# A five-layer graph network on one core: products of the second neighbour sum made within the stretch of the first

## The chip, the core and the metric

The kernel runs on one core of one Trainium2 chip. The metric is the device time of one execution in microseconds, given as the median of the runs shown; lower is better. A profile is one execution recorded by the hardware profiler, and all times from the trace count from its first instruction.

## The reference, cut to what matters

A graph has N = 6250 nodes with 128 features each and E = 106250 directed edges, sorted by destination. Four blocks follow one another, each added to its input and normalised. The change lies in the first block, two mean convolutions:

```python
def _sage_conv(h, src, dst, Wl, bl, Wr):
    msgs = h[src]
    agg = jax.ops.segment_sum(msgs, dst, num_segments=N)
    deg = jax.ops.segment_sum(jnp.ones((src.shape[0],), h.dtype), dst, num_segments=N)
    agg = agg / jnp.maximum(deg, 1.0)[:, None]
    return agg @ Wl.T + bl + h @ Wr.T
...
h = jax.nn.relu(_sage_conv(x, src, dst, W1l, b1l, W1r))
return _sage_conv(h, src, dst, W2l, b2l, W2r)
```

and then `x = _layernorm(x + ...)`. The second block has one symmetric convolution, the third has two, and the fourth has three layers of three weighted hops, each a sum over neighbours with the edges' weights.

## The kernel before, in words

**Sums as dense products.** Nodes are cut into NW = 49 windows of 128. A neighbour sum is a product of node features with a matrix of counts: for a destination, how many edges come from each source. Destinations are taken in NC = 13 chunks, six of 4 windows, three of 3 and four of 4 (RUNS, SHAPE, START: 0, 4, 8, 12, 16, 20, 24, 27, 30, 33, 37, 41, 45). For chunk c, `counted_sum` (L462) walks over the 49 source blocks: it loads the chunk's columns of counts seven blocks at a time on SP's queue (`columns`, L450), casts them from bytes to fp32r two blocks at a time (L478) and multiplies each block with the features. Features are kept as a high and a low part, so each block costs two matmuls (L489) of 512 columns, or 384 for a chunk of three windows. The sum grows in one PSUM bank (`accumulator`, two buffers).

**Where counts come from.** GpSimd writes them. For each of 49 blocks of edge records, `cell` (VectorE) works out the cells and values, and `scatter` (L551) issues 17 indirect DMAs (L555). A chunk's columns may be loaded once the blocks of edges near it have been scattered (`columns` makes the load wait for them). GpSimd's order is written out: `in_line` puts each scatter behind the one before it, first all counts (833), then the matrix of edge weights for the hops (578, L733 to L735), then 48 fetches of edges (`gathered_edges`, L752).

**First sum** (L701 to L731). For each chunk: the next chunk's cells are prepared, degrees are counted (L654), `counted_sum` runs with x's parts (t0hi, t0lo), all casts on ScalarE, and `mean_conv` (L529) turns the sum into h: the sum times w1l, divided by the degree, plus x times w1r, plus the bias; then ReLU, and `split` into t1hi and t1lo. Its argument `also` makes part of the second sum on the way: with the same columns, it adds the products of t1 with the source blocks below START[c], which are known by then (tile `half`, L721 to L725); they are stored in `halves[c]`.

**Second sum** (L777 to L790). Chunk by chunk, with the columns loaded and cast a second time, the source blocks from START[c] on are summed, `evicted` (L496) adds `halves[c]`, and `mean_conv` makes the second convolution: it adds up t1hi and t1lo to h, turns h (`turned`, four transposes, L416, and a copy on ScalarE, L418), multiplies by w2r (`times`, L424) and adds. Then x is added (tile xr, loaded whole by `load_nodes` at L773 on ScalarE's queue), the result is normalised and the next table (t2) is made. Casts alternate between VectorE and ScalarE (`turns`): of seven blocks VectorE takes four.

**Third, fourth and fifth sum** (L811, L829, L842) work in the same way, over all 49 blocks. In the fifth, after chunk c's hop table (L850), `gathered_edges` is called for two windows (L852): GpSimd fetches their edges into tiles gm and ge (L757), and six small VectorE instructions (L761 to L766) unpack them. Those six are held behind L850's instruction of that chunk, so that none comes earlier.

**Hops** (from L1036). Nine hops, whose TensorE order is written out by a planner (class Stream, with costs and due times); part of the destinations go through dense products with the weights' matrix (L1030), the rest through rows that GpSimd gathers (L962).

**What sets the order elsewhere.** Outside the hops a scheduler orders each engine's instructions when the program is built: what is ready by its own reckoning goes first, in the order of the program among those. On the chip each engine then keeps to that order.

Of the kernel before, what the change touches and what calls it, by code (L numbers as in the profile page):

```python
# [360 lines left out]
def usual_way(ctx, tc, a, out, dram, ident, part, first, recs, edges, counts, weights, fills, empty):  # L361
# [97 lines left out]
    def accumulator():  # L459
        return ps_acc.tile([P, CW], F32, name="acc")  # L460

    def counted_sum(pool, c, parts, turns, own=False, wide_bufs=3, slots=None, since=0, also=None):  # L462


        cw, acc, todo, t = width(c), accumulator(), [], None
        step = STEPS
        for s in range(since, NW):
            r = (s - since) % step
            if r == 0:
                t = next(slots) if slots is not None else pool.tile([P, step * CW], U8, name="cols", tag="cols")  # L470
                t = columns(t, c, counts, U8, step, s)
            if not todo:
                n, engine = turns[0]
                turns.append(turns.pop(0))
                wide = pool.tile([P, n * CW], FR, name=f"wide{engine}", tag=f"wide{engine}", bufs=wide_bufs)
                n = min(n, step - r)
                copy = nc.vector.tensor_copy if engine == "v" else nc.scalar.copy
                copy(wide[:, :n * cw], t[:, r * cw:(r + n) * cw])  # L478
                todo = [wide[:, i * cw:(i + 1) * cw] for i in range(n)]
            if own and s == NW - 1:  # L480
                for j, w in enumerate(windows_of(c)):
                    for lhs in parts(w):
                        nc.tensor.matmul(acc[:, j * P:(j + 1) * P], lhs, identr[:], start=False, stop=False)
            cols = todo.pop(0)
            for into, of_block, begin, end in [(acc, parts, since, NW)] + ([also] if also else []):
                if s < end:
                    lhss = of_block(s)
                    for i, lhs in enumerate(lhss):
                        nc.tensor.matmul(into[:, :cw], lhs, cols, start=s == begin and i == 0,  # L489
                                         stop=s == end - 1 and i == len(lhss) - 1)  # L490
        return acc
# [29 lines left out]
    def both(hi, lo):  # L521
        return lambda s: [hi[:, s, :], lo[:, s, :]]

    halves = {c: dram.tile([P, width(c)], F32, name=f"half{c}") for c in range(1, NC)}

    def of(c):
        return SHAPE[c], slice(START[c], START[c] + SHAPE[c])

    def mean_conv(c, acc, wl, wr, bias, hi, lo, more=None):  # L529
        n, ws = of(c)  # L530
        x = new("h", n)
        nc.vector.tensor_add(x[:], hi[:, ws].bitcast(F32), lo[:, ws].bitcast(F32))
        agg = evicted(acc, width(c), more)
        po = times(n, agg, wl)
        y = new("y", n)
        nc.vector.tensor_tensor(y[:], po, per_node(invdeg, ws, D), op=ALU.mult)
        px = times(n, turned(x), wr)
        nc.vector.tensor_add(y[:], y[:], px)
        nc.vector.tensor_add(y[:], y[:], per_feature(bias, n))
        return y  # L540


    queue = []
# [28 lines left out]
    with tc.tile_pool(name="counted", bufs=2) as counted, tc.tile_pool(name="cells", bufs=1) as cells, \  # L572
# [138 lines left out]
        for c in range(NC):  # L711
            n, ws = of(c)
            fetch_chunk(c + 2)
            if c + 4 < NC:
                empty(counts, U8, c + 4, nc.sync)
            count_cells(c + 1)
            for i in sorted(i for i in blocks_near(c) if i in degs):
                degrees(i)
            norms(c)
            also = None  # L720
            if c > 0:  # L721
                also = ps_half.tile([P, CW], F32, name="half"), both(t1hi, t1lo), 0, START[c]
            acc = counted_sum(counted, c, both(t0hi, t0lo), [(2, "s")], slots=slots, also=also)
            if c > 0:
                nc.scalar.dma_start(halves[c][:], evicted(also[0], width(c))[:, :width(c)])  # L725
            y = mean_conv(c, acc, wt["w1l"][:], wt["w1r"][:], wt["b1l"], t0hi, t0lo)
            h = new("h", n)
            nc.vector.tensor_scalar_max(h[:], y[:], 0.0)
            split(t1hi[:, ws], t1lo[:, ws], h[:])
            if c < ND:  # L730
                empty(weights, F32, c, nc.sync)  # L731

# [37 lines left out]
    nc.vector.tensor_copy(wt["wk"][:, 12], ident[:])  # L770
    turns = [(2, "v"), (2, "s"), (2, "v"), (1, "s")]
    xr = tabs.tile([P, NW, D], F32, name="xr", tag="xr")
    load_nodes(nc.scalar, xr, slice(0, NW))  # L773
    with tc.tile_pool(name="counted2", bufs=2) as counted:
        t2 = table("t2", 0, FR)
        slots = columns_room("room1")
        for c in range(NC):  # L777
            n, ws = of(c)
            half = None
            if c > 0:  # L780
                half = sums_room()
                nc.scalar.dma_start(half[:, :width(c)], halves[c][:])
            acc = counted_sum(counted, c, both(t1hi, t1lo), turns, slots=slots, since=START[c])
            y = mean_conv(c, acc, wt["w2l"][:], wt["w2r"][:], wt["b2l"], t1hi, t1lo, half)
            nc.vector.tensor_add(y[:], y[:], xr[:, ws])
            norm(xr[:, ws], y)
            pm = times(n, turned(xr[:, ws]), wt["wconv"][:], DH)
            u = new("u", n, DH)
            nc.vector.tensor_tensor(u[:], pm, per_node(dinv, ws, DH), op=ALU.mult)
            split(t2[:, ws, :DH], t2[:, ws, DH:], u[:])  # L790


        def sym_conv(c, sums, bias, d=D):
            n, ws = of(c)
            r = new("y", n, d)
            nc.vector.tensor_tensor(r[:], sums, per_node(dinv, ws, d), op=ALU.mult)
            nc.vector.tensor_add(r[:], r[:], per_feature(bias, n))
            return r


        def next_parts(c, hi, lo, x):
            n, ws = of(c)
            u = new("u", n)
            nc.vector.tensor_tensor(u[:], x, per_node(dinv, ws, D), op=ALU.mult)
            split(hi[:, ws], lo[:, ws], u[:])

        def summed(c, parts, w):
            return times(SHAPE[c], evicted(counted_sum(counted, c, parts, turns, own=True), width(c)), w)

        t3 = table("t30", 2, FR), table("t31", 3, FR)  # L810
        for c in range(NC):  # L811
            n, ws = of(c)
            agg = evicted(counted_sum(counted, c, lambda s: [t2[:, s, :]], turns, own=True,
                                      slots=slots), width(c))
            pr = bank()
            for j in range(n):
                nc.tensor.matmul(pr[:, j * DH:(j + 1) * DH], agg[:, j * P:(j + 1) * P], stacked[:],
                                 start=True, stop=True)
            r = sym_conv(c, pr[:, :n * DH].rearrange("p (n d) -> p n d", d=DH), wt["bconv"], DH)
            nc.vector.tensor_scalar_max(r[:], r[:], 0.0)  # L820
            po = times(n, turned(r, DH), wt["wlin"][:])
            y = new("h", n)
            nc.vector.tensor_tensor(y[:], po, per_feature(wt["blin"], n), op=ALU.add)
            nc.vector.tensor_add(y[:], y[:], xr[:, ws])
            norm(xr[:, ws], y)
            next_parts(c, *t3, xr[:, ws])

        t4 = table("t40", 0, FR), table("t41", 1, FR)
        for c in range(NC):  # L829
            n, ws = of(c)  # L830
            r = sym_conv(c, summed(c, both(*t3), wt["g1"][:]), wt["gb1"])
            nc.vector.tensor_scalar_max(r[:], r[:], 0.0)
            next_parts(c, *t4, r[:])


        hop_out, hid = table("hop", 2), table("hid", 3)
        stored = [dram.tile([P * NW, D], F32, name=f"stored{i}") for i in range(2)]

        def store(ws, i, t):
            nc.scalar.dma_start(stored[i].rearrange("(p w) d -> p w d", p=P)[:, ws, :], t[:, ws])  # L840

        for c in range(NC):  # L842
            n, ws = of(c)
            r = sym_conv(c, summed(c, both(*t4), wt["g2"][:]), wt["gb2"])
            nc.vector.tensor_add(r[:], r[:], xr[:, ws])
            norm(xr[:, ws], r)
            po = times(n, turned(xr[:, ws]), wt["wk"][:, 0])
            nc.vector.tensor_tensor(hid[:, ws], xr[:, ws], per_feature(wt["bias0"], n), op=ALU.add)
            nc.vector.tensor_add(hid[:, ws], hid[:, ws], po)
            last = nc.vector.tensor_tensor(hop_out[:, ws], xr[:, ws], per_node(dinvw, ws, D), op=ALU.mult)  # L850
            store(ws, 0, hop_out)
            for i in range(2 * c, min(2 * c + 2, NG)):  # L852
                gathered_edges(i, last.ins)
# [549 lines left out]
```

## Time and profile before

| what | value |
|---|---|
| median of 3 runs | 8167.57 us (8165.88 to 8180.15) |
| the profiled execution, its own time | 6165.89 us |
| its span in the trace | 6164.0 us |
| TensorE busy, share of the span | 5392.1 us, 87% |
| GpSimd busy | 4296.6 us, 70% |
| VectorE / ScalarE busy | 3117.1 us / 2142.5 us |
| first sum, to its last eviction | 1254.1 us |
| second sum, from its first unbroken products to its last eviction | 1283.5 to 1476.7 us |
| last scatter of weights begins | 2020.45 us |
| first product of the hops, about | 2316 us |

The profiled execution took 2001.7 us less than the median of the runs; its span doesn't show why. Lines of the profile read as follows. A group names the line, the engine and the operation, then tiles written and read, then a count. PE is TensorE, PEld its weight load, DVE VectorE, ACT ScalarE, POOL GpSimd, SP the engine that only issues DMAs; a q behind a name means the engine's sequencer, which issues DMAs or waits. A line of waits reads: who waited, for whom, microseconds in total, times, the longest.

### The profile page before, as it was taken

The page shows a single profiled execution, that of the slowest core. Times are in us where ns is not written, and L with a number is a line of the kernel's source. Part 1 is how long each engine was busy: PE and PEld are TensorE (multiplying, and loading weights), DVE is VectorE, ACT ScalarE, POOL GpSimd, SP SyncE. Part 2 cuts the span into 40 slices and gives each one's busy share as a digit, 9 for nine tenths or more (in the row PEclk, how much of TensorE's full clock was granted, in tenths as well). Part 3 has the DMA queues.
Part 4 walks back from the last instruction along what each step waited for, and adds up shares of the span by engine and source line. Part 5 has one row for each costly group of instructions (what it writes and reads, how often), then busy time and mean ns, then how long its engine had stood idle before and what let it go on. Part 6 is the DMA issues. An engine that isn't in the chain of part 4 may idle for free.

```text
span 6164.0 us, 74568 instructions
## 1 busy us (share of the span) xinstructions
PE 5392.1 (87%) x20184; PEld 3336.0 (54%) x20184; DVE 3117.1 (51%) x8599; ACT 2142.5 (35%) x4396; POOL 4296.6 (70%) x4207
## 2 busy tenths in 40 slices
PE   1356655889999999999999999999999999999998
PEld 0234443567788784555554555554545555545555
DVE  8274544247955664434445544434355444344466
ACT  1233322445855452323323323323233233233233
POOL 4777777777877306767767747767677477677676
PEclk9688877999999999999999999999999999999999
DMA  9367871154644448999998889999988899998997
GB/s 280 107 189 243 237 194 46 46 147 125 187 130 135 135 136 295 307 308 313 307 316 287 286 287 318 305 312 308 309 299 289 283 320 304 312 310 298 325 319 248
DMA packets 710710, 1525.52 MB, mean 247 GB/s; under 512 B 134918, under 2 KB 344196, under 8 KB 710020
## 3 DMA queue, kind: packets, MB, share of 16 engines
q1 hardware_dynamic: 535728, 1292.14, 62.6%
q0 software_dynamic: 134496, 181.90, 11.0%
q10 hardware_dynamic: 40052, 46.61, 2.2%
q8 instruction: 160, 2.62, 0.2%
q14 instruction: 274, 2.24, 0.1%
HBM read 1332.27 MB, written 187.93 MB: 247 GB/s over the span
## 4 chain that ended last, share of the span: by engine, by line
PE 33%; DMA 27%; POOL 15%; issue 14%; DVE 9%; ACT 2%; POOLq 0%; ACTq 0%; DVEq 0%; SPq 0%
DMA rows<-stored,gsrc 25%; PE acc L1030 20%; POOL weights L555 7%; PE acc L489 5%; POOL counts L555 5%; POOL rows L962 3%; PE gacc L998 2%; ACT both L994 2%; DVE both L995 2%; PE pp L424 1%; PE pd L654 1%; PE half L489 1%; DVE oh L653 1%; PE pp L886 1%; DMA slots<-counts 1%
## 5 line engine op out<-in xcount | busy, mean ns | idle before, releaser
L962 POOL DMA_INDIRECT rows<-stored,gsrc x2736 | 2720.3, 994 | 1229.5 <-issue 348.1
L1030 PE MATMUL acc<-weighed,hop 128*128 128x512 f32 (+1 forms) x7938 | 3492.3, 560 | 2.8 <-DMA weighed<-weights 2.8
L994 ACT ACTIVATE both<-rows,gwgt 128x128 fp32r<-128x128 f32 x2736 | 1075.3, 400 | 2461.1 <-DMA rows<-stored,gsrc 1588.6
L995 DVE SCALAR_TENSOR_TENSOR both<-rows,gwgt,both 128x128 fp32r<-128x128 f32 x2736 | 947.9, 351 | 1876.4 <-ACT both L994 1866.1
L1030 PEld LDWEIGHTS acc<-weighed,hop 128*128 128x128 f32 x7938 | 1326.7, 191 | 988.2 <-issue 750.4
L998 PE MATMUL gacc<-both,oh 128*128 128x256 f32 x2736 | 1743.2, 643 | 4.3 <-issue 2.1
L489 PE MATMUL acc<-wides,t 128*128 128x512 f32 (+1 forms) x2929 | 842.0, 392 | 315.7 <-ACT wides L478 315.6
L555 POOL DMA_INDIRECT counts<-cval,celli x833 | 872.3, 1047 | 269.9 <-issue 244.0
L998 PEld LDWEIGHTS gacc<-both,oh 128*128 128x128 f32 x2736 | 521.8, 191 | 585.1 <-issue 300.7
L555 POOL DMA_INDIRECT weights<-wval,celli x578 | 653.8, 1131 | 176.1 <-issue 176.1
L489 PEld LDWEIGHTS acc<-wides,t 128*128 128x128 f32 x2929 | 540.9, 192 | 427.0 <-ACT wides L478 278.9
L478 ACT CAST wides<-slots 128x1024 fp32r<-128x1024 uint8 (+3 forms) x645 | 527.5, 853 | 633.9 <-DMA slots<-counts 408.6
L489 PE MATMUL acc<-widev,t 128*128 128x512 f32 (+1 forms) x2210 | 608.9, 386 | 21.9 <-DVE widev L478 11.8
L978 DVE TENSOR_TENSOR oh<-iota,gdst 128x640 fp32r<-128x640 f16 x576 | 452.6, 786 | 50.3 <-PE gacc L998 43.9
L489 PEld LDWEIGHTS acc<-widev,t 128*128 128x128 f32 x2210 | 408.6, 189 | 102.8 <-DVE widev L478 25.3
L653 DVE TENSOR_SCALAR oh<-iota,dloc 128x384 bf16<-128x384 f16 x833 | 228.8, 336 | 337.9 <-PE pd L654 337.4
L478 ACT CAST wides<-cols 128x512 fp32r<-128x512 uint8 (+1 forms) x364 | 289.7, 797 | 251.9 <-PE acc L489 223.1
L478 DVE CAST widev<-cols 128x1024 fp32r<-128x1024 uint8 (+1 forms) x364 | 247.8, 686 | 236.2 <-DMA cols<-counts 138.2
L654 PE MATMUL pd<-oh,lw 128*4 128x384 bf16 x833 | 185.8, 339 | 66.3 <-DVE oh L653 65.8
L478 DVE CAST widev<-slots 128x1024 fp32r<-128x1024 uint8 (+1 forms) x281 | 188.2, 681 | 52.9 <-PE acc L489 43.1
L489 PE MATMUL half<-wides,t 128*128 128x512 f32 (+1 forms) x594 | 185.9, 393 | 0.0
L424 PE MATMUL pp<-wk,xT 128*128 128x128 f32 x582 | 95.3, 296 | 84.8 <-ACT xT L418 84.8
(230 smaller groups left out, 2734.1 us busy)
## 6 DMA issues: line engine op xcount, KB each, us to landing
weighed<-weights SPq DMA_DIRECT2D x1296, 512.0 KB
weighed<-weights SPq DMA_DIRECT2D x648, 384.0 KB
slots<-counts SPq DMA_DIRECT2D x175, 448.0 KB
weights<-zeros SPq DMA_DIRECT2D x6, 12544.0 KB
cols<-counts SPq DMA_DIRECT2D x140, 448.0 KB
rows<-stored,gsrc POOLq DMA_INDIRECT x2736
counts<-zeros SPq DMA_DIRECT2D x10, 3136.0 KB
weights<-zeros SPq DMA_DIRECT2D x3, 9408.0 KB
```

Of the source, the lines that this page charges most:

```text
L424: nc.tensor.matmul(pm[:, j * d:(j + 1) * d], xt[:, j * P:(j + 1) * P], w, start=True, stop=True)
L478: copy(wide[:, :n * cw], t[:, r * cw:(r + n) * cw])
L489: nc.tensor.matmul(into[:, :cw], lhs, cols, start=s == begin and i == 0, stop=s == end - 1 and i == len(lhss) - 1)
L555: ins = nc.gpsimd.indirect_dma_start(out=mat[:], out_offset=bass.IndirectOffsetOnAxis(ap=celli[:, i, k:k + 1], axis=0), in_=vals[:, i, k:k ...
L653: nc.vector.tensor_scalar(oh[:], iota[:], dloc[:, k:k + 1], None, op0=ALU.is_equal)
L654: nc.tensor.matmul(acc[:], lw[:, k, :], oh[:], start=k == 0, stop=k == KD - 1)
L962: nc.gpsimd.indirect_dma_start(out=fetched_rows[:, self.slot(self.asked), :], out_offset=None, in_=stored[self.h % 2][:], in_offset=bass.I ...
L978: nc.vector.tensor_tensor(oh[:, :m, :], iota[:, :P].unsqueeze(1).to_broadcast([P, m, P]), gdst[:, i, ks].unsqueeze(2).to_broadcast([P, m, ...
L994: nc.scalar.activation(both[:, :D], x, AF.Copy, scale=w)
L995: nc.vector.scalar_tensor_tensor(both[:, D:], x, w, both[:, :D].bitcast(F32), op0=ALU.mult, op1=ALU.subtract)
L998: nc.tensor.matmul(self.acc[:, j * 2 * D:(j + 1) * 2 * D], self.oh[:, k % HOTS, :], both[:], start=k == 0, stop=k == KG - 1)
L1030: nc.tensor.matmul(acc[:, :cw], tables[h][:, s, :], t[:, s % STEP * cw:(s % STEP + 1) * cw], start=s == 0, stop=s == NW - 1)
```

## The change

`counted_sum` gets an end as well as a start (`until`). `mean_conv` loses the own product, which becomes `plus_product`; `fetched_sums` loads a stored partial sum.

In the first sum, each chunk now also makes its part of the second convolution's own product: x + h w2r + b2l, stored in DRAM as `bases[c]`. And after chunks 8, 9, 10 and 11, two more partial sums follow, those of chunks 0 and 1, 2 and 3, 4 and 5, 6 and 7 of the second convolution: source blocks from START[e] up to KNOWN = START[9] = 33, whose t1 is known after chunk 8. `halves[e]` is added, and the result is stored as `early_parts[e]`. Their columns are loaded and cast for it, all casts on ScalarE.

The second sum then starts at block 33 for chunks 0 to 7 (unchanged for chunks 8 to 12), adds what is stored, and loads `bases[c]` into xr chunk by chunk where it had loaded x whole.

```diff
-    def counted_sum(pool, c, parts, turns, own=False, wide_bufs=3, slots=None, since=0, also=None):
+    def counted_sum(pool, c, parts, turns, own=False, wide_bufs=3, slots=None, since=0, until=NW, also=None):
...
-        for s in range(since, NW):
+        for s in range(since, until):
...
-                n = min(n, step - r)
+                n = min(n, step - r, until - s)
...
-            for into, of_block, begin, end in [(acc, parts, since, NW)] + ([also] if also else []):
+            for into, of_block, begin, end in [(acc, parts, since, until)] + ([also] if also else []):
...
+    KNOWN, AHEAD = START[ND], 8
     halves = {c: dram.tile([P, width(c)], F32, name=f"half{c}") for c in range(1, NC)}
+    early_parts = {c: dram.tile([P, width(c)], F32, name=f"early{c}") for c in range(AHEAD)}
+    bases = {c: dram.tile([P, SHAPE[c], D], F32, name=f"base{c}") for c in range(NC)}
...
+    def fetched_sums(part):
+        t = sums_room()
+        nc.scalar.dma_start(t[:, :part.shape[1]], part[:])
+        return t
+
+    def plus_product(y, x, w, bias):
+        n = y.shape[1]
+        nc.vector.tensor_add(y[:], y[:], times(n, turned(x), w))
         nc.vector.tensor_add(y[:], y[:], per_feature(bias, n))
...
-            y = mean_conv(c, acc, wt["w1l"][:], wt["w1r"][:], wt["b1l"], t0hi, t0lo)
-            h = new("h", n)
+            x = new("h", n)
+            nc.vector.tensor_add(x[:], t0hi[:, ws].bitcast(F32), t0lo[:, ws].bitcast(F32))
+            y = mean_conv(c, acc, wt["w1l"][:])
+            plus_product(y, x[:], wt["w1r"][:], wt["b1l"])
+            h = new("u", n)
             nc.vector.tensor_scalar_max(h[:], y[:], 0.0)
             split(t1hi[:, ws], t1lo[:, ws], h[:])
+
+            plus_product(x, h[:], wt["w2r"][:], wt["b2l"])
+            nc.scalar.dma_start(bases[c][:], x[:])
+            for e in range(2 * (c - ND + 1), 2 * (c - ND + 2)):
+                if 0 <= e < AHEAD:
+                    half = fetched_sums(halves[e]) if e > 0 else None
+                    acc = counted_sum(counted, e, both(t1hi, t1lo), [(2, "s")], slots=slots,
+                                      since=START[e], until=KNOWN)
+                    nc.scalar.dma_start(early_parts[e][:], evicted(acc, width(e), half)[:, :width(e)])
...
-    load_nodes(nc.scalar, xr, slice(0, NW))
...
-            half = None
-            if c > 0:
-                half = sums_room()
-                nc.scalar.dma_start(half[:, :width(c)], halves[c][:])
-            acc = counted_sum(counted, c, both(t1hi, t1lo), turns, slots=slots, since=START[c])
-            y = mean_conv(c, acc, wt["w2l"][:], wt["w2r"][:], wt["b2l"], t1hi, t1lo, half)
+            nc.scalar.dma_start(xr[:, ws], bases[c][:])
+            half = fetched_sums(early_parts[c] if c < AHEAD else halves[c])
+            acc = counted_sum(counted, c, both(t1hi, t1lo), turns, slots=slots,
+                              since=KNOWN if c < AHEAD else START[c])
+            y = mean_conv(c, acc, wt["w2l"][:], half)
```

## The prediction

> **What bounds the kernel now.** I read the slices first, then the waits of the first sum, then GpSimd's own waits, then one table of stretches, then the few microseconds in which GpSimd and VectorE meet.
>
> The slices (40 of 154 us each; the digits are tenths busy):
> ```profile
> PE   1356655889999999999999999999999999999998
> POOL 4777777777877306767767747767677477677676
> ```
> TensorE is half idle in slices 0 to 6 and full from slice 9. GpSimd is the reverse: a level 7 without a break up to slice 12, then nothing before the hops. Who waits up to 1290 us:
> ```profile
> ACT wides L478 <- DMA slots<-counts: 408.6, 13, 62.1
> ...
> PE acc L489 <- ACT wides L478: 315.6, 10, 53.0
> ```
> Each chunk of the first sum waits for its counts, which GpSimd scatters. GpSimd itself, up to 1190 us and then from 1850 to 2021 us, waits for nobody; "issue" is its 0.3 us between two instructions:
> ```profile
> POOL counts L555 <- issue: 243.7, 800, 0.3
> POOL counts L555 <- DVE f L636: 16.7, 2, 16.4
> ```
> ```profile
> POOL weights L555 <- issue: 37.8, 124, 0.3
> ```
> So it runs one queue, at its own pace: 833 scatters of counts, 578 of weights, then the 48 fetches of L757. The table of stretches gives that pace (columns: length, then busy and instructions of PE, PEld, DVE, ACT, POOL, then clock, DMA share, GB/s):
> ```profile
> 1254.00:1283.50 29.50, 6.57 (x26) 5.62 (x25) 7.39 (x12) 2.92 (x5) 22.79 (x22) 0.62 0.95 300
> 1283.50:1477.00 193.50, 192.74 (x1009) 162.23 (x1010) 135.28 (x307) 100.79 (x147) 151.45 (x139) 0.99 0.47 132
> 1477.00:1690.00 213.00, 197.37 (x975) 155.61 (x974) 186.73 (x465) 159.99 (x238) 172.77 (x133) 0.96 0.58 167
> 1690.00:2000.00 310.00, 310.00 (x1531) 265.50 (x1530) 174.37 (x275) 163.74 (x218) 242.36 (x223) 1.00 0.47 133
> ...
> 904.50:954.00 49.50, 2.85 (x11) 0.81 (x10) 4.43 (x18) 1.09 (x2) 37.78 (x39) 0.55 0.13 36
> 1003.00:1043.50 40.50, 1.55 (x9) 0.59 (x8) 2.47 (x11) 0.00 (x0) 30.80 (x32) 0.57 0.08 20
> 1104.00:1131.40 27.40, 1.73 (x10) 0.59 (x8) 2.22 (x8) 0.00 (x0) 20.92 (x22) 0.62 0.11 30
> ```
> Row 2 is the second sum, row 3 the third, row 4 the fourth; the last three are the waits for counts that the early products could fill. One scatter takes 193.5 / 139 = 1.39 us, 213 / 133 = 1.60, 310 / 223 = 1.39, and 49.5 / 39 = 1.27 where VectorE rests. Now the meeting, VectorE's timeline in the fifth sum (start, length, instruction, idle before it):
> ```profile
> 2023.31 0.68 DVE L850 TENSOR_TENSOR hop<-xr,dinvw 128x512 f32<-128x512 f32 x1
> 2024.53 0.21 DVE L761 TENSOR_SCALAR gdst<-gm 128x17 f32<-128x17 f32 x1 [0.53 <-DMA gm<-recs,gat]
> ...
> 2027.00 0.23 DVE L764 TENSOR_SCALAR gdst<-ge 128x2 f32<-128x2 f32 x1 [2.11 <-DMA ge<-edges,gat]
> ...
> 2030.79 0.71 DVE L478 CAST widev<-cols 128x1024 fp32r<-128x1024 uint8 x1
> ```
> and GpSimd's:
> ```profile
> 2020.45 1.09 POOL L555 DMA_INDIRECT weights<-wval,celli  x1 [0.30 <-issue]
> 2021.85 0.99 POOL L757 DMA_INDIRECT gm<-recs,gat  x1 [0.30 <-issue]
> ```
> VectorE finishes the fifth sum's first chunk at 2023.3 us and turns to gathered_edges, whose rows GpSimd began to fetch at 2021.85, straight after its last weight. VectorE already loses 5.5 us there and TensorE 3.9. The two chains arrive together: both must be shortened to gain.
>
> **What the Trainium skill says.** "SBUF — State Buffer", section Who interferes with whom: a VectorE instruction in a 2-port mode holds the port pair that it shares with GpSimd for its whole length. The paces agree in direction: 1.27 us with VectorE at rest, 1.60 with it 88% busy. "TensorE: Matmul & The Clock Gate", section Architectural detail: the array is 16× 32×32, not 1× 128×128: ScalarE and VectorE are strictly first in, first out. The trace agrees: at 1043.52 a cast of chunk 10, held 41.6 us by its counts, stands before the eviction of chunk 9 (1044.47). The same page, What's actually happening: an idle TensorE restarts at half clock for a window of about 3.4 us. After a 24.6 us wait, pairs of 384-wide matmuls here come 0.64 us apart for 6 us, then 0.35.
>
> **The change, part by part.**
> *Products moved.* Chunks 0 to 5 have 33, 29, 25, 21, 17, 13 blocks below 33, so 138 blocks, two matmuls each: 276 of width 512; chunks 6 and 7 have 9 + 6 blocks: 30 of width 384. Pairs start 0.46 us apart at full clock (1215.44, 1215.90), 0.23 each; 384-wide 0.35 a pair, 0.173. 276 x 0.229 + 30 x 0.173 = 63.2 + 5.2 = 68.4 us leave the second sum.
> *Own product moved.* In that stretch w2r's matmuls are busy 11.0 us and the transposes of h 6.3: 17.3 us off TensorE, and three of VectorE's 0.69 us operations per chunk (26 us).
> *Second sum.* TensorE 192.7 - 68.4 - 17.3 = 107 us; VectorE 135.3 - 26 - casts for 153 of 340 blocks (71.6 x 0.45 = 32) = 77 us. TensorE stays the limit: 108 us in place of 193.5, a saving of 85.
> *The load of xr goes* (3.2 MB, ScalarE's queue). ScalarE stood from 1254.7 to 1273.6 behind it, which delayed chunk 12's tail; of the 29.5 us hole some 15 go. In its place come 13 loads and 13 stores of 256 KB and 8 stores of partial sums, 0.33 us of ScalarE each, beside TensorE's work.
> *First sum.* Early pairs follow chunks 8, 9, 10, 11: 124, 92, 60, 30 matmuls = 28.4, 21.1, 13.7, 5.2 us, against waits of 46.7, 40.6, 27.3 and none. Casts on ScalarE alone run 0.93 us per two blocks, as fast as the four matmuls need. Only the last 5.2 us and an own product stay uncovered, and chunk 10's tail (4 us) slips into the wait: +3 us. If the early products came behind the next chunk's first matmul in TensorE's order, up to 68 us would be uncovered. 25 more column loads on SP queue behind chunk 8 to 11's; the fetches of recs are all out by 516 us and from the fourth block of records on cells are ready over 60 us before their scatter, so GpSimd's queue isn't starved.
> *Sum so far:* 85 + 15 - 3 = 97 us: L850 of the fifth sum's first chunk moves from 2023.3 to 1926.
> *What is late next: GpSimd.* It gets no instruction less. From 1192: 79.5 us to the second sum's new start (1271.5) at 1.32 = 60 scatters; 108 us at 1.47 (between 1.39 and 1.60: VectorE's share, 77 / 108 = 0.71, is near the 0.70 of before, and I allow for waits that I don't see) = 73; third sum, fourth sum and fifth's first chunk 370. At 1926 some 578 - 503 = 75 are left; at 1.27 they take 96 us: first fetch at 2022, where it was 2021.85. With 1.39 or 1.60 in the second sum, 2015 to 2029. VectorE holds 4/7 of the casts behind its six small instructions, so TensorE stands too, some 95 us. After it, all is as before, less 2.5 us for a cold restart: **6165.9 + 1.5, so about 6167 to the profiled execution.**
> The runs' median, 8167.57, is 2001.7 us above that execution, and the fastest, 8165.88, is 2000.0 above it; the span (6164.0) and what lies around it (1.9) don't show where. I take that as a constant and forecast 8169.
>
> **Rivals.**
> (1) *The gain is real: 8072.* That needs VectorE's order not to stop at GpSimd, or GpSimd to be early in the timed runs (TensorE slower there by 2000 us before the fifth sum). Against the first: in the order on record chunk 10's cast stands before chunk 9's eviction and chunk 11's before chunk 10's, so whoever made it believed 136 scatters (real: 179 us) to fit in two chunks' work (108 us). By that belief the weights end some 300 us before the fifth sum, and a shift of 97 doesn't move the six instructions. Against the second: a difference so near 2000.0 looks like a constant. 8167.6 - 97 + 1.5 = 8072.
> (2) *Slower: 8193.* GpSimd's chain now sets the end alone, so each microsecond it loses counts. If the second sum drives it at 1.60, that is +7 us; if some 230 scatters from 890 to 1190 us go at 1.37 in place of 1.30 while early products run, +16; cold restart +2.5. Together 8193. It decides once GpSimd's first fetch comes later than 2038. For it: TensorE and VectorE get denser. Against it: the early casts are ScalarE's.
> (3) *The early products don't fill the waits.* Then the first sum is up to 68 us longer, and the stand at GpSimd absorbs it: the same 8169, with a shorter stand.
>
> **How the numbers follow.** About 0.2%, 16 us, is what a measurement of this kernel can tell from no change. GpSimd sets the end (with 3): 0.74, own range 8158 to 8181. Gain: 0.16. Slower: 0.10, half of it past 8184. The range runs from 8146 to 8205, leaving out the gain and a little of the last. Faster 0.18, same 0.71, slower 0.11.
>
> **What would show it.** Right: waits of 46, 40 and 27 us gone from the first sum; second sum near 108 us; a single wait of VectorE L761 for gm of 80 to 100 us in the fifth sum, GpSimd's first L757 within 2015 to 2029. Wrong: no such wait and hops that begin near 2220 us in place of 2316; or scatters over 1.4 us each before 1190.

## The result, and the profile after

The changed kernel takes 8132.74 us (median of 6 runs, 8121.35 to 8137.86), the kernel before 8167.91 us (6 runs beside them): a ratio of 0.9955, 95% interval 0.9943 to 0.9966, so 35 us faster. The forecast of 8169 was wrong, and its range from 8146 did not hold the time.

One thing must be known to read the numbers: the same program takes about 6160 us in some sets of runs (the short level) and 8100 to 8170 us in others (the long level), and all runs of a set agree, so every ratio below is within one set. The profile that the prediction was made from is of the short level (6165.89), the runs that it forecast are of the long one.

The slices of the changed kernel's profiled execution (long level, span 8136.0 us, so a slice is 203 us; slices count from 0):

```profile
PE   1345544311159999978789788887888878978887
POOL 5665456676630001166465564665646636466464
```

This is not the picture of before moved by 2000 us. In slices 7 to 10 TensorE all but stands (3, 1, 1, 1 tenths) while GpSimd is at 6 and 7; in slice 11 GpSimd ends, and from slice 12 on TensorE is at 9. Who waited in the changed kernel up to 1480 us:

```profile
DVE oh L663 <- remote: 333.7, 58, 78.9
ACT wides L478 <- remote: 302.1, 39, 20.9
```

"remote" means that the trace doesn't show who sent the signal. The casts no longer wait for counts, as they did before (408.6 us); they wait for a release that comes late. And the meeting of GpSimd and VectorE in the fifth sum, the core of the prediction, is the other way round here (waits of the changed kernel, 2320 to 3500 us):

```profile
POOL gm L779 <- DVE gwgt L788: 947.2, 7, 846.0
```

GpSimd waits 846 us for VectorE: its last weight went out at 2318 us, and the fifth sum's first chunk comes at 3172. No wait for GpSimd's rows is listed there, so the stand that was to swallow the gain doesn't exist in this execution.

The stretches tell where the 35 us come from (columns: length, then busy and instructions of PE, PEld, DVE, ACT, POOL, clock, DMA share, GB/s). The first row is the scatter of weights; the second runs from GpSimd's last weight to chunk 12's eviction, the end of the first sum; the third from there to the second sum's last eviction. First the kernel before in a traced execution of the long level (8164.4 us), then the changed one:

```profile
1490.00:2288.00 798.00, 127.02 (x290) 66.25 (x289) 32.18 (x101) 31.03 (x39) 556.54 (x572) 0.53 0.03 5
2288.40:2420.70 132.30, 106.49 (x479) 76.92 (x479) 29.68 (x120) 54.57 (x70) 6.70 (x7) 0.88 0.11 30
2420.70:2643.00 222.30, 200.00 (x1035) 168.71 (x1036) 138.64 (x318) 103.10 (x152) 0.00 (x0) 0.93 0.52 154
```

```profile
1530.00:2318.00 788.00, 123.74 (x286) 63.85 (x286) 30.29 (x92) 43.63 (x52) 562.74 (x572) 0.51 0.05 9
2318.40:2513.90 195.50, 170.12 (x782) 125.68 (x782) 42.20 (x158) 100.56 (x125) 6.67 (x7) 0.92 0.20 63
2513.90:2639.00 125.10, 115.08 (x604) 95.90 (x604) 87.81 (x246) 58.19 (x91) 0.00 (x0) 0.95 0.60 188
```

Row 1: some 290 matmuls in almost 800 us, beside 572 scatters, in either kernel. Row 3: 431 matmuls fewer and 97 us less; the prediction had reckoned with 100 for the second sum and the hole ahead of it. Row 2: 303 matmuls and 63 us more. So most of the work that leaves the second sum comes back between GpSimd's end and chunk 12, where TensorE is busy most of the time and nothing hides it. The third to the fifth sum take 8 us less (831 and 823). Together 97 - 63 + 8 = 42 us less from GpSimd's end on. The two traces differ by 28 us, since GpSimd ends 30 us later in the second (2318 against 2288) and the hops, which the change doesn't touch, take 16 us less. Neither is borne out as the change's work: in four other traces with early products GpSimd's last weight goes out at 2287 to 2297 us.

### The profile page after: what moved, and what is told of

It reads as the page before. It is cut to its first block, busy times and chain, and to the rows that moved or that the text cites. A ratio compares the mean times of both kernels' runs of the same rounds, so it can differ in the third digit from the quotient of the medians.

```text
span 8136.0 us, 74691 instructions
## 1 busy us (share of the span) xinstructions
PE 5768.9 (71%) x20184; PEld 3439.5 (42%) x20184; DVE 3043.5 (37%) x8549; ACT 2129.9 (26%) x4437; POOL 4187.5 (51%) x4207
## 5 line engine op out<-in xcount | busy, mean ns | idle before, releaser
L1050 PE MATMUL acc<-weighed,hop 128*128 128x512 f32 (+1 forms) x7938 | 3651.3, 579 | 54.1 <-DMA weighed<-weights 42.4
L1014 ACT ACTIVATE both<-rows,gwgt 128x128 fp32r<-128x128 f32 x2736 | 1022.7, 398 | 3164.8 <-PE gacc L1018 1327.3
L1050 PEld LDWEIGHTS acc<-weighed,hop 128*128 128x128 f32 x7938 | 1367.3, 198 | 1054.6 <-issue 751.6
L489 PE MATMUL acc<-wides,t 128*128 128x512 f32 (+1 forms) x3105 | 963.8, 420 | 767.4 <-issue 399.4
L489 PEld LDWEIGHTS acc<-wides,t 128*128 128x128 f32 x3105 | 610.3, 206 | 971.5 <-issue 467.8
L478 ACT CAST wides<-slots 128x1024 fp32r<-128x1024 uint8 (+3 forms) x687 | 570.0, 863 | 1117.0 <-remote 719.4
L565 POOL DMA_INDIRECT weights<-wval,celli x578 | 568.6, 984 | 227.3 <-issue 227.3
L489 PE MATMUL acc<-widev,t 128*128 128x512 f32 (+1 forms) x2034 | 563.5, 386 | 11.4 <-DVE widev L478 5.3
L478 ACT CAST wides<-cols 128x1024 fp32r<-128x1024 uint8 (+1 forms) x364 | 286.5, 797 | 288.0 <-DMA cols<-counts 155.5
L664 PEld LDWEIGHTS <-lw 128*4 128x4 bf16 x833 | 68.0, 90 | 433.5 <-issue 394.9
```

Of the source, the lines that this page charges most:

```text
L565: ins = nc.gpsimd.indirect_dma_start(out=mat[:], out_offset=bass.IndirectOffsetOnAxis(ap=celli[:, i, k:k + 1], axis=0), in_=vals[:, i, k:k ...
L664: nc.tensor.matmul(acc[:], lw[:, k, :], oh[:], start=k == 0, stop=k == KD - 1)
L1014: nc.scalar.activation(both[:, :D], x, AF.Copy, scale=w)
L1050: nc.tensor.matmul(acc[:, :cw], tables[h][:, s, :], t[:, s % STEP * cw:(s % STEP + 1) * cw], start=s == 0, stop=s == NW - 1)
```

## The experiments

Theory A: at the long level TensorE's hand-overs come late while GpSimd issues indirect DMAs, GpSimd's end starts a clock, and the change is worth what it takes out of the work behind that point, less what it adds there. Theory G: at the short level the prediction's mechanism holds, and the whole gain stands in one wait of VectorE. The rivals are named in the expectations.

### The kernel before, once more

No edit. This set's runs of the kernel before have a median of 8158.4 us (43 runs).

> The kernel before, unchanged, for a second profile. Theory A (in the timed executions the engines hand work to each other slowly as long as GpSimd issues scatters, as the changed kernel's trace shows: 23 of its 40 slices differ from the first profile of before in this way): a span near 8166 us, GpSimd's weights ending near 2300 us, TensorE mostly idle until then, and the second sum only begun after that. Theory B (the slow hand-over comes with the change alone): a span near 6166 us again, as in the first profile.

Measured: 8166.32 us, a span of 8164.4. Its slices:

```profile
PE   1344544111169999978888788887888878978797
POOL 5665446766610000166465564664646636566464
```

This is Theory A's case; Theory B, that only the changed kernel is slow, is out. So the missing 2000 us are not around the execution but inside it, and not spread evenly: weights end at 2288 us (2020 in the first profile), the hops take 4691 us where they took 3848 (2316 to 6164). The groups of this kernel from 1490 to 2288 us:

```profile
L555 POOL DMA_INDIRECT weights<-wval,celli x572 | 556.8, 973 | 241.8 <-issue 241.8
L489 PE MATMUL acc<-wides,t 128*128 128x512 f32 x102 | 59.7, 684 | 344.3 <-ACT wides L478 304.8 <-issue 39.5
...
L478 ACT CAST wides<-slots 128x1024 fp32r<-128x1024 uint8 (+1 forms) x28 | 26.2, 938 | 457.4 <-issue 274.9 <-remote 182.5
```

28 casts with 457 us of idleness ahead of them, 16 us each; a cast itself takes 0.94 us as ever. The matmul waits for the cast, and the cast for the buffer that TensorE's last matmul releases. The trace's semaphore events show which hand-over is late: TensorE's. Each increment was set beside the last matmul before it that could have made it, so a lag read this way is a least one. Between 1300 and 2020 us one in ten of TensorE's recorded increments comes 15.3 us or more after that matmul; in the first profile that figure is 0.015 us, and here too it is 0.014 from 2400 to 3100 us, where GpSimd is idle. ScalarE's and VectorE's own increments are on time in both (0.009 and 0.012 us). The figures are no full count: of TensorE's increments 7605 of 9397 are in this trace, of VectorE's 5622 of 8198, of ScalarE's 2820 of 4389. From 2400 to 3100 us none is missing.

### The own product alone, and the early products alone

Own product alone: no early partial sums; the second sum starts at START[c] as before and adds halves[c].

```diff
-    KNOWN, AHEAD = START[ND], 8
+    KNOWN, AHEAD = START[ND], 0
...
-            half = fetched_sums(early_parts[c] if c < AHEAD else halves[c])
+            half = fetched_sums(halves[c]) if c > 0 else None
...
-                              since=KNOWN if c < AHEAD else START[c])
+                              since=START[c])
```

> The change without the early products: only the own product and x are moved into the first sum, and xr's load goes. Theory A: the second sum runs at full pace after GpSimd's last scatter and is 32 us shorter (17 us of matmuls and transposes, 15 us of the wait behind xr's load); what it adds to the first sum is few instructions: about 8138 us, as much gain as the whole change or more, 25 to 35. Theory C (the gain comes from the early products): within 10 us of 8168.

Early products alone: w2r's product stays in the second sum, and x is loaded whole as before.

```diff
-            plus_product(x, h[:], wt["w2r"][:], wt["b2l"])
-            nc.scalar.dma_start(bases[c][:], x[:])
...
+    load_nodes(nc.scalar, xr, slice(0, NW))
...
-            nc.scalar.dma_start(xr[:, ws], bases[c][:])
...
+            x = new("h", n)
+            nc.vector.tensor_add(x[:], t1hi[:, ws].bitcast(F32), t1lo[:, ws].bitcast(F32))
...
+            plus_product(y, x[:], wt["w2r"][:], wt["b2l"])
```

> The change without the own product: the early products are made in the first sum, w2r's product and the whole load of xr stay in the second. Theory A: 68 us less in the second sum, but they are made while GpSimd scatters, where casts and matmuls take turns slowly, and that delays the first sum by about as much: 8150 to 8185. Theory C: most of the gain of 35, so about 8140.

Measured in the set of 8158.4: own product alone 8144.01 us (ratio 0.9979, 0.9971 to 0.9987), 14 us less by the medians; early products alone 8186.4 us (1.0029, 1.0020 to 1.0038), 28 us more. The first misses its expected 25 to 35 us, the second lies 1 us above what A allowed. Theory C is out: the early products by themselves gain nothing. The parts add up to +14, where the whole change gave -24 and -35 in two other sets. Rows 2 and 3 of the table above, for the own product alone and then for the early products alone:

```profile
2298.00:2434.60 136.60, 116.45 (x528) 83.30 (x526) 33.07 (x133) 55.58 (x71) 6.67 (x7) 0.91 0.12 35
2434.60:2629.00 194.40, 183.24 (x908) 152.21 (x908) 119.28 (x291) 93.56 (x138) 0.00 (x0) 0.96 0.56 170
```

```profile
2297.00:2500.00 203.00, 182.81 (x817) 132.57 (x816) 47.07 (x188) 104.12 (x131) 6.71 (x7) 0.92 0.20 59
2500.00:2672.10 172.10, 140.80 (x747) 118.94 (x747) 113.20 (x282) 71.71 (x111) 0.00 (x0) 0.88 0.51 153
```

Beside the kernel before (132.3 and 222.3 us), the own product alone takes 28 us from the second sum, near the expected 32, and adds 4 ahead of it. The trace is of the fastest of its 22 runs (8112.86), so it places more than the 14 us of the medians. The early products alone take 50 us from the second sum, not 68, and add 71 ahead of it. The two together (97 and 63) thus save 19 us more in the second sum than one by one, and cost 12 less ahead of it. The first can be seen in TensorE's idle time in the second sum: 22 us before, 11 with the own product alone, 31 with the early products alone, 10 with both. TensorE's timeline of the early products alone, just after chunk 12's last products:

```profile
2508.82 2.05 PE L489 MATMUL acc<-widev,t 128*128 128x512 f32 x4 [9.45 <-issue]
...
2527.75 2.08 PE L489 MATMUL acc<-wides,t 128*128 128x512 f32 x4 [12.70 <-ACT wides L478]
```

Two holes of 9.5 and 12.7 us, beside the load of x on ScalarE's queue (issued from 2497.4 on). The kernel before has the same load, issued at 2418 us, and holes of the same sum behind it (9.3, 7.2 and 6.1 us). Only the own product's move takes the load away. Another 7 us of the early products' idle time lie in small waits behind 2640 us, at the last chunks of the second sum, which the kernel before doesn't have. Why the two together cost 12 us less ahead of the second sum isn't shown.

### One scatter of weights in seventeen

The same edit on the kernel before and on the changed one. It leaves out sixteen of every seventeen scatters of weights, so the hops work with an incomplete matrix; their instructions stay.

```diff
-        for k in range(KD):
+        for k in range(KD if dt == U8 else 1):
```

> The kernel before, but of the 17 scatters of each block of weights only the first is issued (34 instead of 578); the other weights are left out. Theory A (TensorE's hand-overs are slow while GpSimd issues scatters, and work runs at full pace only once it has ended): GpSimd's scatters end near 1530 us in place of 2288, what is then left of the first sum takes up to 150 us longer than what was left at 2288, so the whole takes about 7450 to 7550 us. Rival D (the lag of those executions has nothing to do with GpSimd's scatters, it only lies in the same stretch): products would still be slow up to about 2300 us, the whole within 60 us of 8160.

> The changed kernel with the same cut: 34 weight scatters instead of 578, the other weights left out. Theory A: GpSimd ends near 1560 us. The second sum runs at full pace in both kernels, so its saving of 85 us stands, but the early products that come after GpSimd's end (chunks 2 to 7, some 40 us of TensorE) lie uncovered: 30 to 70 us less than the kernel before with the same cut. Rival E (the change is worth what it is worth in the second sum alone, 97 us, once GpSimd is out of the way): 90 to 100 us less.

This set ran at the short level (before: 6160.04 us, 42 runs). Kernel before with the cut: 6151.69 us (ratio 0.999, 0.9984 to 0.9997); changed kernel with it: 6046.16 us (0.9815, 0.9800 to 0.9830). The expected times were for the long level and are not tested here. What is tested is Theory G: the weights' scatters cost the kernel before 8 us and the changed kernel about 107 (6153.46, below). VectorE's timeline of the changed kernel with the cut, in the fifth sum's first chunk:

```profile
1909.00 0.68 DVE L870 TENSOR_TENSOR hop<-xr,dinvw 128x512 f32<-128x512 f32 x1
1909.60 0.17 DVE L783 TENSOR_SCALAR gdst<-gm 128x17 f32<-128x17 f32 x1
```

No wait: GpSimd had fetched the first rows at 1231 us.

The pair was repeated in a set of the long level (before: 8162.47 us):

> Again the kernel before with 34 of its 578 weight scatters, the other weights left out, to meet it where the kernel before takes about 8160 us. There, theory A (TensorE's hand-overs come late while GpSimd issues scatters): about 7450 to 7550. Rival D (the lag is not GpSimd's doing): within 60 us of 8160. Where the kernel before takes about 6160 it says the same as the first time: 6145 to 6160.

> Again the changed kernel with 34 of its 578 weight scatters, the other weights left out. Where the kernel before takes about 8160, theory A: 30 to 70 us less than the kernel before with the same cut, since some early products then lie behind GpSimd's end, uncovered; rival E: 90 to 110 us less. Where the kernel before takes about 6160: 6045 to 6050 again.

Measured: 7473.96 us (0.9153, 0.9136 to 0.9169) and 7444.55 us (0.9109, 0.9085 to 0.9133). 544 scatters out of the way save 689 us, as Theory A said (7450 to 7550), where they save 8 us at the short level; rival D is out. The slices of the kernel before with the cut:

```profile
PE   1253553478999997988888878978978888788787
POOL 5666545620000106646646646566466366465564
```

In slice 8 (1493 to 1680 us) GpSimd falls from 6 to 2 and TensorE rises from 4 to 7. TensorE's increments between 1600 and 2450 us now come within 0.015 us for nine in ten, where it was 10.9 us with the scatters. The change is worth 29 us here, just under the 30 to 70 expected and far from rival E's 90 to 110. Rows 2 and 3 again, first without the change, then with it:

```profile
1542.50:1723.70 181.20, 163.96 (x751) 116.63 (x751) 49.87 (x206) 84.06 (x108) 6.66 (x7) 0.94 0.14 41
1723.70:1945.70 222.00, 199.39 (x1035) 168.31 (x1036) 138.78 (x319) 103.14 (x152) 0.00 (x0) 0.94 0.52 154
```

```profile
1557.60:1805.10 247.50, 231.44 (x1062) 165.97 (x1062) 66.76 (x250) 140.92 (x176) 6.67 (x7) 0.95 0.25 75
1805.10:1929.70 124.60, 114.77 (x604) 95.89 (x604) 87.94 (x247) 58.31 (x92) 0.00 (x0) 0.95 0.61 189
```

So the result's account holds within one set too: 97 us won in the second sum, 66 lost between GpSimd's end and chunk 12's eviction. GpSimd itself ends 15 us later with the change (1558 against 1543), which isn't explained.

### Fewer early sums, and the changed kernel again

```diff
-    KNOWN, AHEAD = START[ND], 8
+    KNOWN, AHEAD = START[ND], 4
```

> The change with AHEAD = 4: early partial sums for chunks 0 to 3 only, those that were made while GpSimd still scattered; chunks 4 to 7 go back to the second sum. Theory A: in the changed kernel the four late ones took 34 us behind GpSimd's end, uncovered, and in the second sum they cost 19 us of TensorE, so this gains some 5 to 15 us on the changed kernel: 40 to 50 us less than before. Rival E (every early product is worth its time in the second sum): 19 us are lost, 10 to 20 us less than before.

> The changed kernel once more, for a second trace and for its time beside the others on the same chip. Both theories: 30 to 40 us less than before. Theory A: GpSimd's last weight scatter within 2290 to 2330 us, the chunks 10 to 12 of the first sum behind it, the second sum's last eviction 310 to 330 us behind it. If the late end of the counts (1522 us, against 1482 to 1489 in three other traces) comes from the early products, it is near 1520 again; if it is chance, near 1490.

In the set of 6160.04: ahead4 6148.56 us (0.9982, 0.9974 to 0.9990), the changed kernel 6153.46 us (0.9985, 0.9977 to 0.9994). The expected times were for the long level again. This is the measurement that the prediction's own level calls for: 7 us less, no gain of 100. The trace of that changed kernel answers the prediction's rows; the stretches after chunk 12's last eviction at 1249 us (second row: the second sum), and the first sum's waits:

```profile
1249.00:1269.00 20.00, 9.01 (x39) 7.16 (x39) 7.62 (x12) 3.96 (x7) 15.42 (x16) 0.75 0.90 260
1269.00:1377.00 108.00, 107.28 (x566) 88.92 (x566) 82.20 (x235) 54.48 (x86) 84.68 (x77) 0.98 0.58 173
1377.00:1583.00 206.00, 198.16 (x1010) 155.84 (x1009) 189.95 (x471) 164.29 (x245) 168.96 (x122) 1.00 0.62 181
```

```profile
ACT wides L478 <- DMA slots<-counts: 316.0, 13, 61.0
PE acc L489 <- ACT wides L478: 284.0, 13, 51.7
```

The second sum takes 108.0 us (193.5 before). And VectorE and GpSimd in the fifth sum, two timelines of the same execution:

```profile
1911.82 0.68 DVE L870 TENSOR_TENSOR hop<-xr,dinvw 128x512 f32<-128x512 f32 x1
2017.32 0.18 DVE L783 TENSOR_SCALAR gdst<-gm 128x17 f32<-128x17 f32 x1 [104.82 <-DMA gm<-recs,gat]
```

```profile
2013.27 0.97 POOL L565 DMA_INDIRECT weights<-wval,celli  x1 [0.30 <-issue]
2014.55 0.99 POOL L779 DMA_INDIRECT gm<-recs,gat  x1 [0.30 <-issue]
```

VectorE reaches L870 111 us earlier than before (2023.3), stands 104.8 us for the rows, and goes on where it went on before.

Both were run again at the long level (before: 8101.41 us):

> AHEAD = 4 once more, to meet it where the kernel before takes about 8160 us. There, theory A: early sums 4 to 7 came behind GpSimd's end and cost 34 us uncovered, 19 us of TensorE in the second sum, so this takes 5 to 15 us less than the changed kernel. Rival E: 10 to 20 us more than the changed kernel. Where the kernel before takes about 6160, as the first time: within 8 us of the changed kernel.

> The changed kernel beside it. Where the kernel before takes about 8160: 25 to 40 us less than before, GpSimd's last weight near 2300 to 2320 us, the second sum from chunk 12's last eviction to its own last one near 125 us. Where the kernel before takes about 6160: 5 to 12 us less than before.

Measured: ahead4 8072.76 us (0.9965, 0.9953 to 0.9978), the changed kernel 8077.53 us (0.9973, 0.9965 to 0.9981). The 5 us between them fit A's 5 to 15, and not E's loss of 10 to 20, but the intervals overlap: that the late early sums gain nothing is shown, that they cost is not. By the traces they cost 16 us ahead of chunk 12's eviction (191.9 against 175.4), where A had reckoned with 34, and save 19 in the second sum (125.1 against 143.7). The changed kernel is 24 us faster than before, just short of its expected 25 to 40; its second sum takes 125 us again, as expected.

### The fetch of edges five chunks later

This takes away what makes VectorE wait: the two windows of edges of a chunk are asked for in the fifth sum's chunks 5 to 10, in place of 0 to 5.

```diff
-            for i in range(2 * c, min(2 * c + 2, NG)):
+            for i in range(2 * max(c - 5, 0), min(2 * max(c - 4, 0), NG)):
```

> The changed kernel, with the calls of gathered_edges moved from the fifth sum's chunks 0 to 5 to its chunks 5 to 10, so that VectorE no longer stops in the first chunk for rows that GpSimd can fetch only after its last weight. Theory G (where an execution takes about 6160 us, the change's 100 us stand in that one wait, from 1902 to 2014 us): if before takes about 6160 here, this takes 6055 to 6075, as GpSimd's weights end near 2014 and the fifth sum near 2212 needs nothing of it sooner. If before takes about 8160 here, GpSimd is through 850 us ahead of the fifth sum, so the move changes nothing: the changed kernel's 8130, within 10 us. Rival H (the gain is lost elsewhere, GpSimd's weights are what the hops wait for): no gain on the changed kernel in either case.

> The same move of gathered_edges on the kernel before, as the control: is it the move by itself that gains? Theory G: in the kernel before VectorE loses only 5.5 us at that wait, so 0 to 8 us less than before, in either case.

The set's kernel before took 6161.86 us. The changed kernel with the move: 6046.26 us (0.9809, 0.9796 to 0.9823), 116 us less and a little below the expected 6055. The kernel before with it: 6155.71 us (0.9988, 0.9981 to 0.9995), within the expected 8 us. So the move frees the change's gain, and only 6 us of the 116 are its own; rival H is out. VectorE's timeline of the changed kernel with the move:

```profile
1911.19 0.68 DVE L870 TENSOR_TENSOR hop<-xr,dinvw 128x512 f32<-128x512 f32 x1
...
2042.79 0.69 DVE L870 TENSOR_TENSOR hop<-xr,dinvw 128x512 f32<-128x512 f32 x1
2043.39 0.17 DVE L783 TENSOR_SCALAR gdst<-gm 128x17 f32<-128x17 f32 x1
```

GpSimd's last weight, at 2029 us (2014 was expected), is now 14 us ahead of VectorE, and five chunks of the fifth sum lie where the wait was.

> The changed kernel with gathered_edges five chunks later, once more. Where the kernel before takes about 8160, theory G: GpSimd is through some 850 us before the fifth sum, so nothing waits there and the move is worth nothing: within 10 us of the changed kernel. Rival (what is gained there comes from the six instructions' place on VectorE, not from GpSimd's end): 80 us or more less than the changed kernel. Where the kernel before takes about 6160: 6046 again.

At the long level (8101.41): 8068.33 us (0.9958, 0.9944 to 0.9973), 9 us less than the changed kernel beside it, within the expected 10. There the wait doesn't exist and the move has nothing to free. Of the versions tried that make the whole result, this one is the fastest at the short level; at the long level it is ahead of the kernel before, and its interval overlaps that of the changed kernel.

## Why the prediction was wrong, by its own steps

**The step that failed is the last: "I take that as a constant."** The 2001.7 us between the profiled execution and the runs were added to a time worked out for an execution of 6166 us. They are no constant around the kernel: some 270 us lie ahead of GpSimd's last weight, some 890 between there and the fifth sum's end (1185 us in place of 296), and 843 in the hops, and they change the order in which the two chains arrive. GpSimd is through at about 2290 to 2320 us and the fifth sum's first chunk at about 3170 to 3185, so the stand of 95 us, which was to swallow the gain, isn't there. The text named this case in its first rival ("TensorE slower there by 2000 us before the fifth sum") and refused it because the difference was near 2000.0. That nearness was chance: between the medians of the kernel before in the sets here it is 1940 to 2008.

**First sum: +3 predicted, and at the level that was forecast +63 measured. This is the second step that failed.** The early products were to fill the waits for counts. At the long level TensorE makes some 290 matmuls in the 800 us up to GpSimd's end, whichever stand in line, so what is put in there pushes other work out: 303 more matmuls lie behind GpSimd's end, in a stretch with no wait of counts to fill. The third rival's cost (up to 68 us) came true there without the stand that was to absorb it.

**The saving in the second sum stood: 100 us predicted with the hole (85 and 15), 97 measured.** The kernel before has the same hole and the same second sum at the long level as in the first profile, 28.8 and 193.5 us:

```profile
2420.70:2449.50 28.80, 6.77 (x25) 5.72 (x25) 7.17 (x11) 2.42 (x5) 0.00 (x0) 0.57 0.93 303
2449.50:2643.00 193.50, 193.23 (x1011) 162.99 (x1012) 131.47 (x307) 100.68 (x148) 0.00 (x0) 0.98 0.45 131
```

With the change both take 125.1 us. So 97 - 63, and 8 in the sums behind, make 42 in the two traces, 35 in the runs. The first rival's 8072 had the sign and the wrong size: it kept the +3 of the first sum and with it all 97.

**Products moved, own product, second sum: right at the level they were read from.** 108 us predicted, 108.0 measured; TensorE 107 and 107.3, VectorE 77 and 82.2. The hole before it, 29.5 us, was to lose 15 and lost 9.5: some ten small loads of weights (L166, L170) on ScalarE's queue still stand ahead of its next instruction there, 11.7 us.

**First sum, at the level it was read from: +3 predicted, -5 measured** (1254.1 to 1249.2): the early products do fill the waits there. With some 12 us more in the sums behind, VectorE was 111 us ahead and not 97.

**What is late next, GpSimd: right at that level.** First fetch predicted for 2022, within 2015 to 2029, measured 2014.55, half a microsecond below; stand of VectorE 95 predicted, 104.8 measured; effect on the whole +1.5 predicted, -7 measured (6153.46 against 6160.04). (How +1.5 follows from a first fetch 0.15 us later and 2.5 us for a restart, the prediction doesn't show.) The scatter's pace in the second sum was taken as 1.47 us and is 108 / 77 = 1.40, with VectorE 76% busy; in the third, 206 / 122 = 1.69 with VectorE 92% busy. That agrees again in direction with the Trainium skill ("SBUF — State Buffer", Who interferes with whom). But VectorE's share isn't all: at the long level a scatter takes 798 / 572 = 1.40 us with VectorE 4% busy. **Rival (2)**, slower scatters, is out: the counts end at 1184.5 us (1190.7 before).

**Left open.** Why TensorE's increments come late while GpSimd issues indirect DMAs in some sets of runs and not in others isn't in these traces: kernel, instructions and bytes are the same. Only that the lag goes when the scatters go is shown. Whether the recording has a part in it isn't tested: increments are missing from the trace of a long execution beside the lag and not where GpSimd is idle, and every run here has a recorded span and clock.

## What to carry to other kernels

When a profile's own time is not that of the runs, the difference is no constant: find out which stages carry it, or forecast both cases, because it decides which of two chains arrives last. Two chains that meet need a look at the point where they meet: a change that shortens one by 100 us gave 7, and moving the six instructions at the meeting gave the rest. And work that is moved into a wait is free only where that wait exists: the early products filled the waits for counts at one level, and at the other they pushed 303 matmuls into the open and cost 63 of the 97 us they saved.

## What was unexpected of the hardware

- With the same program, TensorE's semaphore increments were on time (0.015 us, nine in ten) or up to 15 us late and more, the latter in part of the sets of runs and there while GpSimd issued indirect DMAs: 290 matmuls in 798 us. 544 such DMAs fewer made 8 us in one set and 689 us in another.
- Of the increments that the traces hold, the lag is TensorE's nearly alone: nine in ten of ScalarE's stayed within 0.01 us and of VectorE's within 0.012 in the two kernels' traces (with the early products alone VectorE's figure between 1300 and 2020 us is 1.2). A cast that ran took 0.94 us as ever.
- In the hops of the long executions, where GpSimd gathers rows, one in ten of TensorE's increments is 2.2 us late, and they take 4691 us in place of 3848.
